# Fixing the order of every engine's queue in a planned mixture-of-experts kernel

## The chip, the cores and the metric

The kernel runs on one core of a Trainium2 chip. The metric is the time of one execution in microseconds on the device, taken as the median of several runs. A profile of one execution shows each engine's instructions: PE (TensorE, matrix products; its weight loads are listed as PEld), DVE (VectorE), ACT (ScalarE), POOL (GpSimd) and SP (SyncE, which here only issues transfers). Each engine works through its own queue in order; semaphores let it wait for the others.

## The reference

The input `x` is 16 sequences of 256 tokens with 256 features. Eight experts and one shared expert are all applied to every token, in float32, and the result is added to `x`:

```
g = einsum('bsd,edf->ebsf', h, Wg)            # E = 8, D = 256, F = 1024
u = einsum('bsd,edf->ebsf', h, Wu)
expert_outs = einsum('ebsf,efd->ebsd', silu(g) * u, Wd)
expert_output = einsum('be,ebsd->bsd', gating_probs, expert_outs)
shared = (silu(h @ Sg) * (h @ Su)) @ Sd
out = x + (1 - sg) * expert_output + sg * shared
```

There is no routing: the gate is a number for each sequence and expert, so the work is the same for any input.

## The kernel before, in words

The work is cut into 72 units `(e, half, g)`: nine experts (the shared one is the ninth), two halves of the 1024 hidden columns, and four groups `g` of four sequences. `g` runs innermost, so four units in a row use the same weights; I call the (expert, half) pair a weight set. There are 18 sets.

**One unit.** The up projection (`unit_up`) forms four token blocks times four column blocks for both weight matrices, `m = 0` (Wg) and `m = 1` (Wu). It does it with fewer products than the plain way. Four "diagonal" steps (`diagonal`) use the raw weights in the tile `wb` and the inputs in `xd`, and collect in the one PSUM bank `D`. Twelve "off-diagonal" steps (`offdiagonal`) use combined weights `wp` and combined inputs `xp`: one product goes to a bank `M`, the VectorE adds it to a sum `s` that GpSimd made from the diagonal results `p` and `q` (tiles `pq`), and writes the sum into a bank `X` (the row `X<-M,s`, which I call the seed); two more products are then added on top of the seed by TensorE. A finished bank goes through silu on ScalarE (`sg`), and the VectorE multiplies the `Wu` bank with it and with the gate `coef` into `h`. The down projection (`unit_down`) of the unit before runs between these products: seven products `dn` instead of eight, with weights `wd`, copied to `ev` by ScalarE and added to a total in HBM by a transfer that GpSimd issues.

**Weights.** `load_base` fetches one set's `wb` for one `m` in two transfers of 256 KB, `u` and `v`. Then GpSimd and VectorE rewrite parts of it in place (rows `wb<-wb`), and `make_pair` builds six `wp` tiles from each. There are four `wb` buffers, so a set's weights are fetched about one set ahead of their use.

**What sets the order.** The kernel does not issue its instructions directly. Every step is an `Op` with an engine, an estimated length, a lag (the time from its end until others may use its result), a rank, the steps that it depends on, and the buffers that it takes or uses. `Plan.run` walks through time with these estimates: an engine that is free takes the ready step of lowest rank, and TensorE is held to the exact rank order. A transfer's lag is `3 + kb / 150` us unless one is given; `load_base` gives 12 for all sets but the first. At the end `run` calls `emit` on all steps in the planned order. The recording layer below (the tile framework) then finds the data dependences and puts the instructions of each engine into an order of its own, by its own estimates; so the queues of the built program are not the planned ones. In the plan the load `v` depends on `u` and so stands 12 us later; in the built program only one other transfer stands between them on SP.

Of the kernel before, what the change touches and what calls it, by code (L numbers as in the profile page):

```python
# [46 lines left out]
class Plan:  # L47
# [18 lines left out]
    def add(self, engine, length, rank, emit, deps=(), new=(), uses=(), lag=None):  # L66
        lag = self.HOP if lag is None else lag
        op = Op(engine, length, lag, rank, emit, deps, list(new), list(uses))
        for b in [*op.new, *op.uses]:
            b.users += 1  # L70
        self.ops.append(op)
        return op

    def run(self):
        free = self.slots
        ready = {}
        serial = {id(op): n for n, op in enumerate(self.ops)}
        for op in self.ops:
            ready.setdefault(op.engine, [])
        at = {id(op): 0.0 for op in self.ops}  # L80
        idle = {e: 0.0 for e in ready}
        events = []
        for op in self.ops:
            if not op.missing:
                heapq.heappush(events, (0.0, serial[id(op)], 0, op))
        order = []
        left = len(self.ops)
        line = sorted((op.rank, serial[id(op)]) for op in self.ops if op.engine == "PE")
        at_line = 0
        turn = {tag: deque() for tag in free}  # L90
        for op in sorted(self.ops, key=lambda op: (op.rank, serial[id(op)])):
            for b in op.new:
                turn[b.tag].append(b)
        now = 0.0
        while left:
            while events and events[0][0] <= now + 1e-9:
                _, _, kind, op = heapq.heappop(events)
                if kind == 0:
                    heapq.heappush(ready[op.engine], (op.rank, serial[id(op)], op))
                elif kind == 1:  # L100
                    for b in [*op.new, *op.uses]:
                        b.users -= 1
                        if not b.users:
                            free[b.tag].append(b.tile)
            for e in ready:
                if idle[e] > now + 1e-9 or not ready[e]:
                    continue
                held, took = [], None
                while ready[e]:
                    item = heapq.heappop(ready[e])  # L110
                    if e == "PE" and item[:2] != line[at_line]:
                        held.append(item)
                        break
                    if all(free[b.tag] and turn[b.tag][0] is b for b in item[2].new) and all(
                        b.tile is not None for b in item[2].uses
                    ):
                        took = item[2]
                        for b in took.new:
                            b.tile = free[b.tag].popleft()
                            turn[b.tag].popleft()  # L120
                        break
                    held.append(item)
                for item in held:
                    heapq.heappush(ready[e], item)
                if took is None:
                    continue
                at_line += e == "PE"
                end = now + took.length
                idle[e] = end
                order.append(took)  # L130
                left -= 1
                heapq.heappush(events, (end, serial[id(took)], 2, took))
                heapq.heappush(events, (end + took.lag, serial[id(took)], 1, took))
                for a in took.after:
                    a.missing -= 1
                    t = end if a.engine == e == "PE" else end + took.lag
                    at[id(a)] = max(at[id(a)], t)
                    if not a.missing:
                        heapq.heappush(events, (at[id(a)], serial[id(a)], 0, a))
            if left:  # L140
                if not events:
                    raise RuntimeError("the plan has come to a stop")
                now = max(now, events[0][0])
        for op in order:
            op.emit()
        return now


@with_exitstack
def kernel(  # L150
# [28 lines left out]
    nc = tc.nc  # L179
# [8 lines left out]
    const = ctx.enter_context(tc.tile_pool(name="const", bufs=1))  # L188
    psum = ctx.enter_context(tc.tile_pool(name="psum", bufs=1, space=bass.MemoryType.PSUM))
    dram = ctx.enter_context(tc.tile_pool(name="dram", bufs=1, space=bass.MemoryType.DRAM))  # L190

    plan = Plan()
    add = plan.add
# [69 lines left out]
    def load(rank, dst, src, kb, deps=(), new=(), uses=(), lag=None):  # L263
        return add("SP", 0.6, rank, lambda: nc.sync.dma_start(dst(), src), deps, new, uses, lag=lag or 3 + kb / 150)  # L264

    def tt(engine, rank, o, a, b, op, n, deps, new=(), uses=(), slow=1.0):
        eng, length = (nc.vector, dve(n) * slow) if engine == "DVE" else (nc.gpsimd, pool(n))
        return add(engine, length, rank, lambda: eng.tensor_tensor(o(), a(), b(), op), deps, new, uses)  # L268
# [9 lines left out]
    def sources(e):  # L278
        return (Wg[e], Wu[e], Wd[e]) if e < E else (Sg, Su, Sd)
# [5 lines left out]
    def load_base(m, e, half, rank):  # L285
        b = Buf("wb", f"wb_{m}_{e}_{half}")
        src = [
            sources(e)[m][ts(part, P), ts(half, 4 * P)].rearrange("p (c q) -> p c q", q=P)
            for part in range(2)
        ]  # L290
        lag = None if rank < 0 else 12
        u = load(rank, lambda: b[:, :, 0, :], src[0], 256, [], [b], lag=lag)
        v = load(rank, lambda: b[:, :, 1, :], src[1], 256, [u], [], [b], lag=lag)
        ops = []
        for i, t in enumerate(POINTS):
            r, x_ = (lambda i=i: b[:, i, 1, :]), (lambda i=i: b[:, i, 0, :])
            if t == 0:
                op = v
            elif abs(t) == 1:
                op = tt("POOL", rank + 1, r, r, x_, ALU.add if t > 0 else ALU.subtract, P, [u, v], uses=[b])  # L300
            else:
                op = stt(rank + 1, r, x_, float(t), r, ALU.add, P, [u, v], uses=[b])
            ops.append(op)
        base[m, e, half], baseop[m, e, half] = b, (u, ops)
# [210 lines left out]
    def diagonal(n, m, unit, a, rank, pq, consume):  # L515

        e, half, g = unit
        w, (u, rops) = base[m, e, half], baseop[m, e, half]
        xb, xo = xd[g, a], xdop[g, a]
        name = f"{m}_{n}_{a}"  # L520
        bank = Buf("D", f"D_{name}")
        p_, q_ = pq
        new = a == 0
        ps, qs = [], []
        for h, i in enumerate((2 * a + 1, 2 * a)):
            ps.append(
                mm(
                    MM, rank + 1 / 8 + h / 100, lambda h=h: bank[:, h, :], lambda i=i: w[:, i, 0, :],
                    lambda i=i: xb[:, i % 2, :], h == 0, True, h == 1, [u, xo[i][0], *ps],
                    [bank] if h == 0 else [], [w, xb] if h == 0 else [w, xb, bank],  # L530
                )
            )

        sp = add(
            "ACT", act(2 * TB), rank + 0.3,
            lambda: nc.scalar.copy(p_[:, 2 - 2 * a : 4 - 2 * a, :], bank[:, :, :]), ps,  # L536
            [p_] if new else [], [bank] if new else [bank, p_],
        )
        for h, i in enumerate((2 * a + 1, 2 * a)):
            qs.append(  # L540
                mm(
                    MM, rank + 9 / 8 + h / 100, lambda h=h: bank[:, h, :], lambda i=i: w[:, i, 1, :],
                    lambda i=i: xb[:, 2 + i % 2, :], False, True, True, [rops[i], xo[i][1], sp],
                    [], [w, xb, bank],
                )
            )
        ops = {}
        for h, i in enumerate((2 * a + 1, 2 * a)):
            first = new and h == 0
            ops[i] = tt(  # L550
                "DVE", rank + 1.5, lambda i=i: q_[:, i, :], lambda h=h: bank[:, h, :],
                lambda i=i: p_[:, 3 - i, :], ALU.subtract, TB, [*qs, *ops.values()],
                [q_] if first else [], [bank, p_] if first else [bank, p_, q_],
            )
        consume(bank, [*ops.values()], rank + 1.6, [(2 * a + 1, 2 * a + 1), (2 * a, 2 * a)])
        return ops

    def offdiagonal(n, m, unit, k, rank, pq, pqops, consume):
# [322 lines left out]
    for n, unit in enumerate(units):  # L881
# [32 lines left out]
            finish(g, pieces, r0 + 2 * W + 1)  # L914
        else:
            unit_down(n, unit, hb, hops)
    plan.run()


# [36 lines left out]
```

## Time and profile before

| | us |
|---|---|
| runs | 2586.86, 2596.26, 2596.96; median 2596.26 |
| profiled execution, its own time | 2590.57 |
| its span, first to last instruction | 2588.8 |
| granted TensorE clock, mean | 0.997 |
| PE busy in the span | 2525.8 |
| PE weight loads, DVE, ACT, POOL busy | 1819.9, 1846.1, 788.8, 1800.1 |

The profiled execution took 1.8 us more than its span and 5.7 us less than the median of the runs. Busy time of PE is from modelled ends of matmuls, and includes matmuls that run while the clock is low; so a PE that is busy is not always at its best.

### The profile page before, as it was taken

The numbers are of one execution on the slowest core, as the hardware profiler recorded it, in microseconds if no ns is written. First come the engines' busy times: TensorE is split into PE (matmuls) and PEld (weight loads), VectorE is DVE, ScalarE is ACT, GpSimd is POOL, SyncE is SP. The second block draws the span as 40 slices with busy tenths as digits, with TensorE's granted clock in tenths as the row PEclk, the third lists the DMA queues.
The fourth block names the chain that finished last, engine by engine and source line by source line (L and its number), as shares of the span: only waits on it lengthen the run. The fifth ranks groups of instructions, "written<-read, shape, count | busy, mean of one in ns | idle before, by whom it ended". The sixth has DMA issues, their size and how long they took to land.

```text
span 2588.8 us, 30164 instructions
## 1 busy us (share of the span) xinstructions
PE 2525.8 (98%) x9644; PEld 1819.9 (70%) x9644; DVE 1846.1 (71%) x3272; ACT 788.8 (30%) x1367; POOL 1800.1 (70%) x1638
## 2 busy tenths in 40 slices
PE   8899999999999999999999999999999999999998
PEld 4667777767776777777676767777776777677766
DVE  6886766777676767676677767676766667776797
ACT  2333333333333333333333333333332333333310
POOL 5686767667676767676766757686767677676654
PEclk9999999999999999999999999999999999999999
DMA  6545666656666656666665665665666666666652
GB/s 196 197 162 154 171 157 164 162 158 164 166 157 164 157 158 169 154 170 156 163 161 161 161 166 157 167 154 158 171 154 164 161 165 158 163 163 177 174 188 90
DMA packets 179087, 421.47 MB, mean 163 GB/s; under 512 B 15057, under 2 KB 84193, under 8 KB 170225
## 3 DMA queue, kind: packets, MB, share of 16 engines
q1 hardware_dynamic: 159280, 294.70, 34.4%
q0 software_dynamic: 19648, 124.86, 26.2%
q8 instruction: 75, 1.23, 0.2%
q14 instruction: 84, 0.68, 0.1%
HBM read 276.90 MB, written 142.61 MB: 162 GB/s over the span
## 4 chain that ended last, share of the span: by engine, by line
PE 88%; DMA 6%; DVE 3%; issue 1%; POOL 1%; SPq 0%; ACT 0%; DVEq 0%; POOLq 0%
PE dn L509 31%; PE X L509 27%; PE D L509 17%; PE M L509 14%; DMA wb<-in_L_cond_Wg_dram 4%; DVE h L273 1%; DMA wb<-in_L_cond_Sg_dram 1%; DVE X L268 1%; DVE h L268 1%; SPq L264 0%; DMA total<-ev 0%; POOL wp L268 0%; PE dn L829 0%; DVE xp L268 0%; DMA wb<-in_L_cond_Wu_dram 0%
## 5 line engine op out<-in xcount | busy, mean ns | idle before, releaser
L268 POOL TENSOR_TENSOR s<-pq,pq 128x512 f32<-128x512 f32 x852 | 1191.3, 1402 | 483.2 <-DVE X L268 471.8
L509 PE MATMUL dn<-h,wd 128*128 128x512 f32 x1988 | 1018.0, 594 | 1.4 <-DVE xd L273 1.4
L509 PE MATMUL X<-xp,wp 128*128 128x256 f32 x3408 | 878.2, 380 | 37.0 <-DVE X L268 37.0
L268 DVE TENSOR_TENSOR X<-M,s 128x512 f32<-128x512 f32 x852 | 586.7, 692 | 435.4 <-PE M L509 227.9
L509 PEld LDWEIGHTS X<-xp,wp 128*128 128x128 f32 x3408 | 645.7, 190 | 254.5 <-issue 103.4
L509 PE MATMUL D<-xd,wb 128*128 128x256 f32 x2272 | 584.5, 380 | 2.6 <-ACT pq L536 2.2
L509 PEld LDWEIGHTS M<-xp,wp 128*128 128x128 f32 x1704 | 324.4, 190 | 346.0 <-issue 338.2
L509 PE MATMUL M<-xp,wp 128*128 128x256 f32 x1704 | 508.1, 380 | 0.1
L729 ACT COPY ev<-dn 128x512 f32<-128x512 f32 x476 | 278.8, 586 | 708.6 <-PE dn L509 708.6
L509 PEld LDWEIGHTS D<-xd,wb 128*128 128x128 f32 x2272 | 431.5, 190 | 67.3 <-ACT pq L536 3.9
L273 DVE SCALAR_TENSOR_TENSOR h<-X,coef,sg 128x256 f32<-128x256 f32 x852 | 375.9, 475 | 122.2 <-PE X L509 107.8
L268 DVE TENSOR_TENSOR h<-h,h 128x512 f32<-128x512 f32 x426 | 448.0, 1052 | 1.9
L509 PEld LDWEIGHTS dn<-h,wd 128*128 128x128 f32 x1988 | 377.6, 190 | 54.8 <-DVE xd L273 2.2
L607 ACT ACTIVATE sg<-X 128x512 f32<-128x512 f32 x434 | 259.1, 597 | 441.8 <-PE X L509 278.0
L536 ACT COPY pq<-D 128x512 f32<-128x512 f32 x284 | 166.5, 586 | 501.7 <-PE D L509 498.3
L268 DVE TENSOR_TENSOR pq<-D,pq 128x256 f32<-128x256 f32 x568 | 218.9, 416 | 25.5 <-PE D L509 25.3
L268 POOL TENSOR_TENSOR h<-h,h 128x512 f32<-128x512 f32 x142 | 197.8, 1393 | 3.6 <-DVE h L268 2.9
L743 POOL DMA_DIRECT2D total<-ev x128 | 112.8, 881 | 66.4 <-ACT ev L729 63.7
L268 POOL TENSOR_TENSOR wb<-wb 128x128 f32<-128x128 f32 x72 | 48.5, 684 | 129.1 <-DMA wb<-in_L_cond_Wg_dram 98.0
L273 DVE SCALAR_TENSOR_TENSOR h<-D,coef,sg 128x256 f32<-128x256 f32 x284 | 134.8, 475 | 0.0
L273 DVE SCALAR_TENSOR_TENSOR wp<-wb,wp 128x256 f32<-128x256 f32 x108 | 106.6, 998 | 29.9 <-POOL wp L268 24.0
L607 ACT ACTIVATE sg<-D 128x512 f32<-128x512 f32 x142 | 84.4, 594 | 98.5 <-DVE pq L268 98.5
(68 smaller groups left out, 561.1 us busy)
## 6 DMA issues: line engine op xcount, KB each, us to landing
xp<-keep_p SPq DMA_DIRECT2D x408, 384.0 KB, 3.9
total<-ev POOLq DMA_DIRECT2D x68, 1024.0 KB, 7.9
xd<-keep_d SPq DMA_DIRECT2D x136, 512.0 KB, 3.5
total<-ev POOLq DMA_DIRECT2D x68, 768.0 KB, 6.9
keep_p<-xp SPq DMA_DIRECT2D x24, 384.0 KB, 2.7
wb<-in_L_cond_Wg_dram SPq DMA_DIRECT2D x33, 256.0 KB, 5.5
wb<-in_L_cond_Wu_dram SPq DMA_DIRECT2D x33, 256.0 KB, 4.2
wd<-in_L_cond_Wd_dram SPq DMA_DIRECT2D x64, 128.0 KB, 2.7
```

What stands on the lines that cost most here:

```text
L268: return add(engine, length, rank, lambda: eng.tensor_tensor(o(), a(), b(), op), deps, new, uses)
L273: lambda: nc.vector.scalar_tensor_tensor(o(), a(), c() if callable(c) else c, b(), ALU.mult, op),
L509: lambda: nc.tensor.matmul(o(), w(), mv(), start=start, stop=stop, skip_group_check=onto),
L536: lambda: nc.scalar.copy(p_[:, 2 - 2 * a : 4 - 2 * a, :], bank[:, :, :]), ps,
L607: lambda: nc.scalar.activation(b[:, :, :], bank[:, :, :], AF.Silu), deps, [b], [bank],
L729: lambda ev=ev, at=at, bank=bank: nc.scalar.copy(ev[:, at, :], bank.tile.rearrange("p a t -> p (a t)")),
L743: nc.gpsimd.dma_start(total[g][part], ev[:, 0:k, :], accum_op=ALU.add)
```

## The change

Four things change. `Plan.run` returns the planned order, and the loop that emits it ties each instruction, by an order edge that carries no semaphore, to the one emitted before it on the same engine. The recording layer can then no longer exchange instructions of one engine; the planned order is the order of every queue. The lag of `load_base`'s transfers goes from 12 to 14 us. `v` no longer depends on `u`, so the plan issues both together. In `diagonal` the rank of the two subtractions that make `q` goes from `rank + 1.5` to `rank + 0.6`, and that of what follows them from `rank + 1.6` to `rank + 0.7`, which puts them ahead of other VectorE and ScalarE work that is ready at the same time.

```diff
@@ Plan.run
-        for op in order:
-            op.emit()
-        return now
+        return order
@@ tile_cond_moe_resid_kernel
+    same_queue = mybir.DependencyInfo(mybir.DependencyClass.NoSync, mybir.DependencyReason.DATA)
@@ load_base
-        lag = None if rank < 0 else 12
+        lag = None if rank < 0 else 14
         u = load(rank, lambda: b[:, :, 0, :], src[0], 256, [], [b], lag=lag)
-        v = load(rank, lambda: b[:, :, 1, :], src[1], 256, [u], [], [b], lag=lag)
+        v = load(rank, lambda: b[:, :, 1, :], src[1], 256, [], [], [b], lag=lag)
@@ diagonal
             ops[i] = tt(
-                "DVE", rank + 1.5, lambda i=i: q_[:, i, :], lambda h=h: bank[:, h, :],
+                "DVE", rank + 0.6, lambda i=i: q_[:, i, :], lambda h=h: bank[:, h, :],
                 lambda i=i: p_[:, 3 - i, :], ALU.subtract, TB, [*qs, *ops.values()],
                 [q_] if first else [], [bank, p_] if first else [bank, p_, q_],
             )
-        consume(bank, [*ops.values()], rank + 1.6, [(2 * a + 1, 2 * a + 1), (2 * a, 2 * a)])
+        consume(bank, [*ops.values()], rank + 0.7, [(2 * a + 1, 2 * a + 1), (2 * a, 2 * a)])
@@ end of the kernel
-    plan.run()
+    last = {}
+    for op in plan.run():
+        at = len(nc.cur_bb.bb.instructions)
+        op.emit()
+        for ins in nc.cur_bb.bb.instructions[at:]:
+            if ins.engine in last:
+                tc.add_manual_dep(ins, last[ins.engine], same_queue, reason="plan")
+            last[ins.engine] = ins.name
```

## The prediction

> **What bounds the kernel now.** I began with the page, whose first lines say which engine is full.
>
> ```profile
> PE 2525.8 (98%) x9644; PEld 1819.9 (70%) x9644; DVE 1846.1 (71%) x3272; ACT 788.8 (30%) x1367; POOL 1800.1 (70%) x1638
> ...
> PE 88%; DMA 6%; DVE 3%; issue 1%; POOL 1%; SPq 0%; ACT 0%; DVEq 0%; POOLq 0%
> ```
>
> TensorE is the bound, and the change removes no matmul. So I need the time that no order can take away. The chain of waits gives what one record costs when TensorE runs on (`PE X L509 x4` takes 0.86 us, `PE dn L509 x2` 0.86): 0.215 us for 256 columns, 0.43 for 512. With the counts of the page: 1988 dn x 0.43 + (3408 X + 2272 D + 1704 M) x 0.215 = 2442 us, and some 60 for the first and last units' own forms. That is about 2503 of a span of 2588.8: an order can win at most some 86 us. The windows show where they lie (us; PE, PEld, DVE, ACT, POOL busy; then clock, DMA share, GB/s).
>
> ```profile
> 0.00:160.00 160.00, 139.54 (x504) 89.78 (x505) 123.80 (x216) 46.60 (x92) 108.04 (x127) 0.98 0.57 190
> ...
> 290.00:404.00 114.00, 114.00 (x439) 83.08 (x438) 81.50 (x145) 36.26 (x63) 83.40 (x75) 1.00 0.58 155
> ...
> 2440.00:2589.00 149.00, 134.70 (x545) 96.31 (x543) 120.13 (x196) 22.24 (x38) 74.26 (x54) 1.00 0.50 153
> ```
>
> Within a weight set TensorE is never idle (114.00 of 114.00). The start loses 20.5 us, the end 14.3, and the rest is at the 15 places between 277 and 2243 where a new set's weights are fetched. Windows of 14 us around these places:
>
> ```profile
> 551.20:565.20 14.00, 11.96 (x42) 8.49 (x41) 8.34 (x16) 3.54 (x6) 7.21 (x8) 0.88 0.59 169
> 693.00:707.00 14.00, 12.01 (x50) 9.14 (x49) 9.71 (x17) 3.54 (x6) 8.77 (x9) 1.00 0.74 187
> ...
> 1393.20:1407.20 14.00, 12.06 (x42) 8.42 (x42) 9.03 (x17) 3.54 (x6) 7.97 (x8) 0.88 0.71 186
> ...
> sum 210.00, PE 181.57 PEld 136.40 DVE 143.50 ACT 53.09 POOL 129.15; mean PE 12.10 PEld 9.09 DVE 9.57 ACT 3.54 POOL 8.61
> ```
>
> The list of waits names what TensorE lacked, and what its supplier lacked; the timeline of one place shows the order of events.
>
> ```profile
> PE X L509 <- DVE X L268: 37.0, 22, 2.8
> ...
> POOL wb L268 <- DMA wb<-in_L_cond_Wg_dram: 98.0, 13, 11.6
> DVE wb L273 <- DMA wb<-in_L_cond_Wg_dram: 89.6, 15, 7.2
> ```
>
> ```profile
> 546.14 0.38 SPq L264 DMA_DIRECT2D wb<-in_L_cond_Wg_dram  x1
> ...
> 548.36 0.70 DVE L268 TENSOR_TENSOR X<-M,s 128x512 f32<-128x512 f32 x1 [1.38 <-POOL s L268]
> 555.46 0.29 DVE L273 SCALAR_TENSOR_TENSOR wb<-wb 128x128 f32<-128x128 f32 x1 [6.40 <-DMA wb<-in_L_cond_Wg_dram]
> 555.67 0.87 DVE L273 SCALAR_TENSOR_TENSOR h<-X,coef,sg 128x256 f32<-128x256 f32 x2
> 556.46 1.29 DVE L268 TENSOR_TENSOR X<-M,s 128x512 f32<-128x512 f32 x2
> ...
> 557.20 1.73 PE L509 MATMUL X<-xp,wp 128*128 128x256 f32 x4 [2.04 <-DVE X L268]
> ```
>
> The second load of Wg is issued at 546.14. VectorE reaches the rewrite of these weights at 549.06, 2.9 us later, and stands there until the load lands, 9.2 us after its issue. GpSimd does the same. The new weights are for the next set, and sets are 140 us apart, but the seed `X<-M,s` is behind them in VectorE's queue, and TensorE, which had work for 6 us, runs dry.
>
> **The change part by part.** *The tie with the longer lag, and `v` issued beside `u`.* In the planned order, which is now each queue's order, I counted the matmuls between the second load of a set and its first use. For Wg: 28 of 256 columns and 8 of 512 before VectorE's rewrite (28 x 0.43 + 8 x 0.86 = 18.9 us), and 28.4 before GpSimd's. For Wu, 14.6 and 21.1. The slowest landing of a `wb` load in the trace is 10.0 us. So the rewrite no longer waits, and nothing is queued behind a wait.
>
> [...] The trace has a DMA share of 0.70 to 0.80 in most of the 15 windows, against 0.58 within a set. [...]
>
> What the 15 places cost: 210.00 - 181.57 = 28.4 us without a matmul. After a gap the first group of four takes 1.13 us instead of 0.86 in the chain: 13 x 0.27 = 3.5. And twice the clock fell: 2 x (1 - 0.88) x 14 = 3.4. [...] The rows show 0.88 after gaps near 2 us, so I count it: 35.3. I keep 3 us as still lost in one place or another: -32.
>
> *The start.* `v` of the first set moves up from the tenth transfer on SP to the second, so GpSimd's rewrite, which started at 14.5 us, can start near 6. VectorE now makes two `wp` tiles ahead of the first `h`, where it made six; TensorE's `PE M L509 <- DVE h L273: 4.5, 2, 3.3` should go. Against it: 512 KB more stand ahead of the last two inputs (2.2 us at the first window's 234 GB/s; TensorE waited for them at 11.5), and `oms<-coef` is now VectorE's first step. It needs a transfer that landed at 9.75 (issued at 2.35, 7.4 to landing), and with its 0.42 and 0.71 us it delays the first copy from 8.1 to 10.9. I take these two, which overlap, at 1.5: net -3. For the rest of the first 160 us the trace shows no such order; VectorE is 87% to 96% busy there. Bounds: all of the remaining waits for VectorE gone (-8), or as much lost (+6). I take -1, since the work is the same.
>
> *The diagonal's ranks.* No instruction is added: 568 subtractions (416 ns) and 284 products (475 ns) move up in VectorE's queue, and 142 silus in ScalarE's. TensorE waits only 2.6 us in all for bank `D`, so a gain is bounded by that. The cost is bounded by what is delayed: up to 2 x 0.42 + 2 x 0.48 = 1.8 us for a seed behind them. Within a set VectorE waits for TensorE's `M` (227.9 us in all), so it is ahead of TensorE and covers this: 0.
>
> *Order edges* carry no semaphore and add no instruction: 0. *SP's queue:* the four `wd` loads of a set now stand in one block (an issue like the one at 546.14 takes 0.38 us), with the `xp` loads behind them. Those are planned 19 us ahead (median) and land in 3.8 (8.3 at most): 0. *The end:* the same reading of the totals; a store that lands after 9.5 us is planned with 8, so a wait there stays. Bounds -5 and +5; 0.
>
> **Sum.** 2590.6 (the profiled execution) - 32 - 3 - 1 = 2554.6. The median of the runs is 5.7 us above that execution, the fastest run 3.7 below it; I add 2: **2557 us**, 1.5% less than the median.
>
> **The rivals.** *Slower: the fixed queue makes VectorE late in every unit.* The diagonal's four steps come ahead of a seed 284 times (4 a unit, 71 units). It decides as soon as more than (36 + 13) / 284 = 0.17 us a time is not covered. At 0.25 it gives 2590 + 71 - 36 = 2625. For it: a fixed queue can't step around a step that is late, and TensorE had 98%. Against it: 114.00 of 114.00 within a set, with VectorE waiting for TensorE. 10%.
> *Partly given back.* GpSimd has about 14 us of weight work a set (48.5 + 105.0 + 94.7 us in its groups over 18 sets); freed of its wait it may hold up the sums `s` that a seed needs. If about half of the 32 us stay as such waits: 2575. 12%.
> *Nothing moves.* The plan's estimates are off where it matters, and its own order waits at the same places or at the start, for the 36 us that it saves: 2590. 8%.
>
> **How the numbers follow.** The main case has 70%; its own range is 2541 to 2570. About 0.5% (13 us) is what a measurement of this kernel can tell from no change. Faster by more than that: main and partly, 0.82. Within: 0.09, the last rival and the edge of another. Slower: 0.09. The range from 2536 (35 at the sets, 12 at the start, 7 at the end) to 2592 leaves out most of the slow rival and the ends of the others.
>
> **What would show it.** Right: no wait of VectorE or GpSimd on `wb<-in_L_cond_Wg_dram` over 1 us after 160 us; `PE X L509 <- DVE X L268` below 8 us; PE 13.8 or more in the 14 us windows, with clock 1.00. The start: no gap of 3 us before the first `M` products near 27 us. Wrong: PE below 113.5 of 114 within a set (the slow rival), or GpSimd's `s` as the releaser of seeds at the sets (partly given back).

## The result, and the profile after

| | before | after |
|---|---|---|
| median of five runs (us) | 2594.71 (2586.86 to 2596.96) | 2561.45 (2560.55 to 2563.84) |
| ratio, 95% interval | | 0.9877 [0.986, 0.9893] |
| profiled execution (us) | 2590.57 | 2560.55 |
| its span | 2588.8 | 2558.8 |
| clock, mean | 0.997 | 0.997 |

The change takes 1.2% off. The profiled span falls by 30.0 us. The windows say where (after: us; PE, PEld, DVE, ACT, POOL busy; clock, DMA share, GB/s; the last window ends with the span, as it did before):

```profile
0.00:160.00 160.00, 138.09 (x496) 89.91 (x497) 116.29 (x208) 45.58 (x90) 98.13 (x116) 0.97 0.54 182
290.00:404.00 114.00, 114.00 (x438) 82.68 (x436) 86.45 (x151) 36.75 (x65) 81.10 (x79) 1.00 0.59 155
2410.00:2559.00 149.00, 133.34 (x534) 96.04 (x533) 119.53 (x192) 20.93 (x36) 69.69 (x52) 0.98 0.49 152
```

Within a set TensorE is still never idle. The start loses 21.9 us (20.5 before) at a clock of 0.97 (0.98); the end loses 15.7 (14.3) at 0.98 (1.00). Both ends are therefore a little worse. All of the gain is at the 15 places where a set's weights are fetched. Windows of 14 us that begin 3 us behind the issue of the first load (those of the prediction begin 7 to 8 us behind it):

```profile
546.80:560.80 14.00, 14.00 (x55) 10.26 (x54) 7.45 (x15) 4.83 (x9) 6.64 (x7) 1.00 0.93 232
684.60:698.60 14.00, 14.00 (x56) 10.26 (x55) 7.40 (x15) 4.88 (x9) 6.64 (x7) 1.00 0.94 230
...
sum 210.00, PE 210.00 PEld 154.07 DVE 111.54 ACT 72.83 POOL 98.88; mean PE 14.00 PEld 10.27 DVE 7.44 ACT 4.86 POOL 6.59
```

TensorE fills 210.00 of 210.00 us, where it had 181.57, and the clock is 1.00 in each. These windows end ahead of the rewrites, but over the whole stretch from 160 to 2240 us TensorE is busy 2079.80 of 2080.00 us too. The timeline of the place that the prediction showed, again after the change, has no wait in it:

```profile
543.75 2.12 SPq L264 DMA_DIRECT2D wb<-in_L_cond_Wg_dram  x2
...
565.70 0.70 DVE L273 SCALAR_TENSOR_TENSOR wb<-wb 128x128 f32<-128x128 f32 x1
```

Both loads are issued by 545.87, and VectorE comes to their rewrite 20 us later, not 2.9 us later. The list of waits (us in total, times, longest) agrees:

```profile
PE dn L401 <- DVE xd L273: 8.1, 3, 4.2
PE X L509 <- DVE X L268: 7.4, 5, 2.6
POOL wb L268 <- DMA wb<-in_L_cond_Wg_dram: 2.6, 1, 2.6
```

TensorE's wait for seeds falls from 37.0 to 7.4 us. GpSimd's wait for Wg falls from 98.0 to 2.6, once, at the start; VectorE's, 89.6 before, is gone from the list. What grows most on TensorE is `PE dn L401 <- DVE xd L273`, from 4.0 to 8.1 us, and this is at the start.

### The profile page after: what moved, and what is told of

The parts are those of the page before. It is cut to its first block, busy times and chain, and to the rows that moved or that the text cites. A ratio compares the mean times of both kernels' runs of the same rounds, so it can differ in the third digit from the quotient of the medians.

```text
span 2558.8 us, 30286 instructions
## 1 busy us (share of the span) xinstructions
PE 2521.2 (99%) x9644; PEld 1822.6 (71%) x9644; DVE 1894.3 (74%) x3272; ACT 778.3 (30%) x1367; POOL 1721.5 (67%) x1638
## 3 DMA queue, kind: packets, MB, share of 16 engines
q8 instruction: 76, 1.25, 0.2%
## 5 line engine op out<-in xcount | busy, mean ns | idle before, releaser
L268 POOL TENSOR_TENSOR s<-pq,pq 128x512 f32<-128x512 f32 x852 | 1147.9, 1376 | 523.1 <-DVE X L268 502.9
L273 DVE SCALAR_TENSOR_TENSOR h<-X,coef,sg 128x256 f32<-128x256 f32 x852 | 394.8, 478 | 214.3 <-PE X L509 163.8
L268 DVE TENSOR_TENSOR h<-h,h 128x512 f32<-128x512 f32 x426 | 468.6, 1126 | 0.0
L268 POOL TENSOR_TENSOR wp<-wb 128x128 f32<-128x128 f32 x216 | 140.4, 661 | 0.0
L273 DVE SCALAR_TENSOR_TENSOR h<-D,coef,sg 128x256 f32<-128x256 f32 x284 | 134.5, 474 | 0.0
L273 DVE SCALAR_TENSOR_TENSOR wp<-wb,wp 128x256 f32<-128x256 f32 x108 | 88.3, 819 | 0.0
```

Of the source, the lines that this page charges most:

```text
L273: lambda: nc.vector.scalar_tensor_tensor(o(), a(), c() if callable(c) else c, b(), ALU.mult, op),
```

## Experiments

Times are medians; each ratio is to runs of the kernel before on the same chip. Diffs are against the changed kernel unless they say otherwise.

**The edges alone (`tie_only`), against the kernel before:** `load_base` and `diagonal` are as they were.

```diff
-        for op in order:
-            op.emit()
-        return now
+        return order
...
+            if ins.engine in last:
+                tc.add_manual_dep(ins, last[ins.engine], same_queue, reason="plan")
+            last[ins.engine] = ins.name
```

> The kernel before with the order edges alone: v still depends on u, the lag is 12, and the diagonal's ranks are the old ones. Theory 1 (the recording layer put the rewrite of the weights too early in the queues; the planned order cures it): in this plan the first rewrite stands at least 12.5 us of matmuls behind the second load, and the slowest landing measured is 10.3 us, so the waits at the weight sets go and the time is 2555 to 2572 us. Theory 2 (the pairing of u and v and the longer lag do it): 2585 to 2597. Theory 3 (the diagonal's ranks do it): 2585 to 2597.

Measured: 2560.12 us, ratio 0.987 [0.9855, 0.9884]. The edges give all of the gain. With the landing time of 12 us that the plan had already, the planned order keeps the rewrites far enough behind their loads. TensorE's wait for seeds is as short as in the changed kernel:

```profile
PE X L509 <- DVE X L268: 5.8, 4, 2.8
```

**The loads alone (`loads_only`), against the kernel before:** no edges.

```diff
-        lag = None if rank < 0 else 12
+        lag = None if rank < 0 else 14
...
-        v = load(rank, lambda: b[:, :, 1, :], src[1], 256, [u], [], [b], lag=lag)
+        v = load(rank, lambda: b[:, :, 1, :], src[1], 256, [], [], [b], lag=lag)
```

> The kernel before with the lag of 14 and with v freed from u, but no order edges and the old ranks. Theory 1: the recording layer still orders the queues by its own estimates, the rewrite stands about 3 us behind the load again, PE X waits about 2 us at each of 15 sets: 2580 to 2600 us. Theory 2: 2555 to 2575.

Measured: 2592.99 us, ratio 0.9996 [0.9985, 1.0008]: nothing. Both waits stay:

```profile
DVE wb L273 <- DMA wb<-in_L_cond_Wg_dram: 89.3, 15, 7.9
PE X L509 <- DVE X L268: 39.2, 23, 3.6
```

The queues are not the plan's, so the plan's estimate of a landing does not reach them.

**The old ranks of the diagonal (`ranks_old`):**

```diff
-                "DVE", rank + 0.6, lambda i=i: q_[:, i, :], lambda h=h: bank[:, h, :],
+                "DVE", rank + 1.5, lambda i=i: q_[:, i, :], lambda h=h: bank[:, h, :],
...
-        consume(bank, [*ops.values()], rank + 0.7, [(2 * a + 1, 2 * a + 1), (2 * a, 2 * a)])
+        consume(bank, [*ops.values()], rank + 1.6, [(2 * a + 1, 2 * a + 1), (2 * a, 2 * a)])
```

> The changed kernel with the diagonal's ranks put back to 1.5 and 1.6. Theory 1: the sets stay free of waits, TensorE is full within a set in either case, 2556 to 2567 us. Theory 3 (the ranks carry the gain): over 2580.

Measured: 2564.42 us, ratio 0.9886 [0.9871, 0.99], against 0.9877 with the new ranks. The ranks' 3 us lie inside the intervals.

**The same fixed queues with the rewrite put close behind its load (`early_rewrite`).** The plan is told that a set's load lands 2 us after its issue. By the planned order TensorE then has 2.6 us of matmuls between the load and VectorE's rewrite.

```diff
-        lag = None if rank < 0 else 14
+        lag = None if rank < 0 else 2
```

> The changed kernel, its order edges included, with a lag of 2 us for the weight loads in place of 14: VectorE's rewrite then stands 2.6 us of matmuls behind the load of Wg, as it did in the kernel before (2.9 us). Theory 1: the wait comes back although the queues are fixed, VectorE stands 5 to 7 us at each of 15 sets and TensorE loses about 2 us there, 2583 to 2600 us. Rival (it is the fixed order as such that helps, by fewer semaphore waits on VectorE and GpSimd): 2556 to 2568.

Measured: 2622.08 us, ratio 1.0112 [1.0094, 1.013], slower than the kernel before. From its timeline:

```profile
556.72 2.13 SPq L264 DMA_DIRECT2D wb<-in_L_cond_Wg_dram  x2
...
568.43 0.29 DVE L273 SCALAR_TENSOR_TENSOR wb<-wb 128x128 f32<-128x128 f32 x1 [7.05 <-DMA wb<-in_L_cond_Wg_dram]
...
570.17 1.68 PE L509 MATMUL X<-xp,wp 128*128 128x256 f32 x4 [2.69 <-DVE X L268]
```

The wait that the change removed is back at the same place: VectorE stands 7.05 us, then TensorE 2.69. So a fixed order gains nothing by being fixed; the distance between load and rewrite in it decides. This kernel loses more than the kernel before, and more than I expected. Its trace says where. From 160 to 2300 us TensorE is idle for 39.7 us; the kernel before lost 28.4 at the sets, the changed kernel loses 0.2. The clock also falls at nine of the sets, where it fell at two before: the group of four at 570.17 takes 1.68 us, where 1.13 follows a gap at the full clock, and the 14 us from 569 have a clock of 0.88. Over the span the mean clock is 0.990 against 0.997 in the changed kernel; 0.007 of the span is an estimated 18 us. Idle time and clock make up about 58 of the 66 us between the two spans (2625.0 and 2558.8).

**Edges on VectorE's and GpSimd's queues only (`tie_dve_pool`), and on VectorE's only (`tie_dve`):**

```diff
+            if ins.engine not in (mybir.EngineType.DVE, mybir.EngineType.Pool):
+                continue
```

> The changed kernel, but order edges are laid on VectorE's and GpSimd's queues alone; TensorE, ScalarE and SyncE are ordered by the recording layer again. Theory 1 (what counts is how far behind a weight load VectorE's and GpSimd's rewrites stand in their own queues): 2555 to 2567 us, no wait of either on wb<-in_L_cond_Wg_dram over 1 us after 160 us, and PE 13.8 or more in the 14 us windows at the sets. Theory 2 (the gain needs the matmul order too, since TensorE's order is what kept the layer's order and the plan's apart): 2580 to 2592, with waits of TensorE on X or D in every set.

```diff
+            if ins.engine != mybir.EngineType.DVE:
+                continue
```

> The changed kernel, but order edges are laid on VectorE's queue alone; GpSimd's is the recording layer's. Theory 1 (either engine standing at a load in its queue is enough to starve TensorE, since a seed needs GpSimd's s as well): GpSimd waits some 7 to 11 us for wb<-in_L_cond_Wg_dram at most sets, VectorE then waits for s, and the time is 2572 to 2590. Theory 2 (only VectorE's wait reached TensorE; GpSimd's s is made far enough ahead of its use to hide 10 us): 2556 to 2566, with GpSimd's wait still in the list but PE near 14.00 in the windows at the sets.

Measured: with both queues tied 2551.01 us, ratio 0.9832 [0.9817, 0.9847], better than with all tied, and 4 us below the range that I gave. With VectorE's alone 2634.88 us, ratio 1.0158 [1.0143, 1.0173]: far slower than either theory allowed. It is not the wait at the load: GpSimd still stands at Wg for 64.3 us in 10 waits, but VectorE's wait for `s` is 68.5 us, as with both queues tied (68.8), and TensorE's wait for seeds is only 10.5. In its place stands another wait, about two a set:

```profile
PE D L509 <- ACT sg L607: 50.0, 33, 3.6
```

The mean clock is 0.990 (0.999 with both tied); by the difference an estimated 24 us go there. One of the waits:

```profile
283.24 0.86 POOL L743 DMA_DIRECT2D total<-ev  x1
...
284.86 5.83 DVE L268 TENSOR_TENSOR h<-h,h 128x512 f32<-128x512 f32 x1
...
285.08 1.54 POOL L268 TENSOR_TENSOR h<-h,h 128x512 f32<-128x512 f32 x1
...
289.18 0.95 POOL L268 TENSOR_TENSOR wp<-wp,wb 128x256 f32<-128x256 f32 x1
...
290.61 0.41 DVE L268 TENSOR_TENSOR pq<-D,pq 128x256 f32<-128x256 f32 x1
...
291.70 1.13 PE L509 MATMUL D<-xd,wb 128*128 128x256 f32 x4 [2.25 <-ACT sg L607]
```

VectorE's `h<-h,h` takes 0.68 us when it is alone. Here it takes 5.83 us. It starts 0.8 us behind an accumulating transfer that GpSimd issued, and ends when the GpSimd instructions behind that issue, which follow each other without a pause, have run out (290.13). The step `pq<-D` waits behind it, the silu for `pq`, TensorE for the silu. In this kernel 30 VectorE operations take over 4 us, about two a set; with GpSimd's queue tied as well there is one, at the start, and in the kernel before there is one. My reading is that the layer's order of GpSimd's queue puts the weight work right behind the issue, while VectorE's fixed queue cannot step round. Length alone is no loss: in the changed kernel 64 VectorE operations between 160 and 2400 us take 2.2 to 4 us, none did before, and TensorE stays full. The next experiments ask what holds the operation.

**The first set's plain stores issued by SyncE (`sp_store`).** The changed kernel has the same event twice in its start (at 101.63 and 143.06 us). The first stands ahead of TensorE's longest wait:

```profile
100.54 0.57 POOL L741 DMA_DIRECT2D total<-ev  x1 [2.65 <-ACT ev L729]
...
101.63 4.18 DVE L273 SCALAR_TENSOR_TENSOR xp<-xd,xp 128x256 f32<-128x256 f32 x1
...
104.27 1.26 POOL L268 TENSOR_TENSOR h<-h,h 128x512 f32<-128x512 f32 x1
...
110.71 0.65 PE L401 MATMUL dn<-ident,xio 128*128 128x128 f32 x4 [4.19 <-DVE xd L273]
```

```diff
-                        nc.gpsimd.dma_start(total[g][part], ev[:, 0:k, :])
+                        nc.sync.dma_start(total[g][part], ev[:, 0:k, :])
...
-                    "POOL", 0.9, r + 0.1, store, [*evops, totalop.get((g, part))], uses=[ev], lag=8.0
+                    "SP" if first else "POOL", 0.6 if first else 0.9, r + 0.1, store, [*evops, totalop.get((g, part))], uses=[ev], lag=8.0
```

> The changed kernel, but the first set's stores of the totals (plain writes of ev, one for each total) are issued by SyncE and not by GpSimd. In the changed kernel two VectorE operations right behind such an issue take 4.18 us instead of 0.4 to 0.9, and TensorE has gaps near them (110.7 and 150 us). Theory 1 (GpSimd's issue of a plain store holds VectorE's operation up): both long operations are gone and the time falls by 2 to 6 us, to 2555 to 2560. Theory 2 (the length is due to something else at that place, or the gaps near it come from the order): long operations stay at 99 to 105 and 140 to 145 us, or go without any gain; 2560 to 2563.

Measured: 2559.54 us, ratio 0.9864 [0.9848, 0.9881]. Both operations of 4.18 us are gone (the longest near the first is 1.79). TensorE's longest wait for `xd` falls from 4.2 to 2.4 us. PE is 141.43 in the first 160 us against 138.09, but the clock is lower, 0.96 against 0.97 there and 0.95 against 0.98 in the last 149 us, and of the 3.3 us little arrives: 1.9 us less than the changed kernel, inside the intervals. So the long operations go with the issue, but a gain in time is not shown.

**The first step of VectorE and the last inputs (`head_order`):**

```diff
-    coef_op = add("DVE", 0.8, -2, make_coef)
+    coef_in = add("COEF", 0.01, -3, lambda: None, lag=9.7)
+    coef_op = add("DVE", 0.8, -2, make_coef, [coef_in])
...
-        v = load(rank, lambda: b[:, :, 1, :], src[1], 256, [], [], [b], lag=lag)
+        v = load(rank, lambda: b[:, :, 1, :], src[1], 256, [u] if rank < 0 else [], [], [b], lag=lag)
```

> The changed kernel, but in the plan the gate's step on VectorE (oms<-coef) is held until 9.7 us, behind the first copies, and in the first weight set alone v depends on u again, as it did before the change. Theory 1 (the predicted -4 us of the start was lost because VectorE's first step waits 8.3 us for the gate's transfer and the last inputs come later): first copies near 8.3 instead of 10.1 us, the first products near 13.2 instead of 15, and 1.5 to 3 us less in all: 2558 to 2560. Theory 2 (the start is bounded by VectorE's amount of work in the first 160 us, so an earlier first product is given back by gaps later): 0, within 1.5 us of the changed kernel, with PE in the first 160 us still 137.5 to 139.

Measured: 2560.18 us, ratio 0.9868 [0.9853, 0.9882]. The first copy moves from 10.11 to 8.55 us and the first `X` product from 14.98 to 14.06, but PE in the first 160 us is 138.06 against 138.09, at a clock of 0.95 against 0.97. What comes earlier is given back before 160 us, as the second theory said; that VectorE's amount of work is the reason is not shown by it.

**What holds VectorE (`port`, then `port_issue`).** Two small programs, which compute nothing of the reference, measured by one profile each. Part of the first (the second operation of VectorE is the one that is timed):

```diff
+                nc.scalar.copy(t, last)
+                for i in range(n):
+                    nc.gpsimd.tensor_tensor(g[i], t, big[:, 512:1024], ALU.mult)
...
+                nc.vector.tensor_tensor(first, lead, t, ALU.mult)
...
+                    nc.vector.tensor_tensor(o, first, big[:, 1024:1536], ALU.mult)
```

> A small program of its own: none of the reference is computed, the output holds products of the input. In each trial GpSimd is given 0, 1, 2, 4 or 8 products of 128x512 from SBUF in a row, and VectorE, just behind their start, one operation of 128x512: two operands in SBUF (tensor_tensor, or the same with a scalar), one operand in PSUM and one in SBUF, or one operand in SBUF. Theory 1 (VectorE's operation with both operands in SBUF can't start until GpSimd's run of back-to-back instructions ends, which is what made h<-h take 4.2 to 7.2 us in the kernel with VectorE's edges alone, and xp<-xd,xp 4.18 us at 101.63 us of the changed kernel): with two SBUF operands it takes about 0.7 us alone, and about 1.3 us more for each further GpSimd product, some 10 us behind 8; with an operand in PSUM, or a single operand, it stays near 0.6 to 0.7. Theory 2 (it waits for one GpSimd instruction at most): never more than about 2 us, whatever the run. Theory 3 (the length came from the DMA issue or the stores nearby): 0.7 in every trial.

Measured: with two SBUF operands 0.69 us alone and 1.13 to 1.20 beside 1, 2, 4 or 8 products alike; with one in PSUM 0.69 throughout; with a single SBUF operand 0.43 alone and 0.86 to 0.93 beside GpSimd, which no theory of mine had. The first theory was wrong and the second held: beside back-to-back products alone VectorE's operation took at most 0.51 us more (1.20 against 0.69), and no more beside eight than beside one. The second program puts the issue of a transfer first:

```diff
+        if issue == "plain":
+            emit(nc.gpsimd.dma_start, total, ev)
+        elif issue == "accum":
+            emit(nc.gpsimd.dma_start, total, ev, accum_op=ALU.add)
         for i in range(n):
             emit(nc.gpsimd.tensor_tensor, g[i], t, big[:, 512:1024], ALU.mult)
```

> A second small program of its own, without any of the reference: as the first, but in each trial GpSimd may issue a transfer of 128x2048 to HBM first (none, a plain store, or an accumulating one), then 0, 1, 4 or 8 products of 128x512; VectorE starts its operation with two SBUF operands behind one, two or four short PSUM operations of 0.7 us. In two last trials VectorE's operation has one operand in PSUM. In the kernel with VectorE's edges alone and in the changed kernel, the operations of over 2.2 us nearly all start within 4 us of such an issue and end 4.7 to 6.6 us behind its end. Theory 1 (an issue from GpSimd with products queued behind it holds VectorE's two-operand operation until most of those have run): no more than 1.2 us without an issue, 0.7 to 1.2 with an issue and no product behind it, and 3 to 6 us with an issue and 4 or 8 products. Theory 2 (the issue alone holds it, products or not): 3 to 6 us with 0 products too. Theory 3 (neither; what held it was something else of the kernel, such as the semaphores between GpSimd's own rewrites): never over 2 us.

Three trials of its timeline, all with 8 products: no issue; a plain store; the store again, with VectorE's operand in PSUM:

```profile
32.16 10.25 POOL L31 TENSOR_TENSOR g<-ev,big 128x512 f32<-128x512 f32 x8 [0.73 <-ACT ev L31]
32.73 1.25 DVE L31 TENSOR_TENSOR none<-big,ev 128x512 f32<-128x512 f32 x1
...
109.29 0.58 POOL L31 DMA_DIRECT2D total<-ev  x1 [1.64 <-ACT ev L31]
109.64 10.60 DVE L31 TENSOR_TENSOR plain<-big,ev 128x512 f32<-128x512 f32 x1
109.89 9.79 POOL L31 TENSOR_TENSOR g<-ev,big 128x512 f32<-128x512 f32 x8
...
296.48 9.80 POOL L31 TENSOR_TENSOR g<-ev,big 128x512 f32<-128x512 f32 x8
296.93 0.68 DVE L31 TENSOR_TENSOR bnk<-bank,ev 128x512 f32<-128x512 f32 x1
```

Behind an issue VectorE's operation lasts 0.68 us with no product behind it, 2.04 with one, 5.73 with four and 10.60 with eight. Started later, behind four short operations, it takes 3.53 with four and 8.41 with eight: it ends with the run each time, 0.5 to 0.6 us behind the last product. An accumulating transfer does the same (6.02 and 10.88). The first theory holds, and more strongly than I wrote it: VectorE waits for the whole run, up to the eight products tried. Its bound of 1.2 us without an issue was too low (1.25 to 1.73 while products ran).

**All edges but TensorE's (`tie_no_pe`), and the smallest version (`dve_pool_min`: the kernel before plus edges on VectorE and GpSimd):**

```diff
+            if ins.engine == mybir.EngineType.PE:
+                continue
```

> The changed kernel with the edges on every queue but TensorE's. Theory 1 (the 10 us between the changed kernel and the one with edges on VectorE and GpSimd alone are TensorE's: tied, it stands behind a step whose input is late at the start and at the end, where the layer's order lets another matmul go first): 2549 to 2554 us. Theory 2 (they come from ScalarE's or SyncE's edges, late copies or late transfers): 2558 to 2563.

> The kernel before with one edit: edges on VectorE's and GpSimd's queues. Lag, the place of v and the diagonal's ranks are as before the change. Theory 1 (only where the two engines' rewrites stand counts; the rest of the change carries nothing): 2548 to 2555 us. Theory 2 (the ranks or the longer landing time carry part of it once TensorE's order is the layer's): 2556 to 2575.

Measured: 2554.49 us, ratio 0.9865 [0.9848, 0.9881], and 2546.56 us (2546.17 to 2549.27), ratio 0.9835 [0.982, 0.9849], the fastest of all. The smallest version lies 1.4 us below the range that I gave. It has the ratio of `tie_dve_pool` (0.9832), so the lag, `v` and the ranks add nothing there either. Its two ends:

```profile
0.00:160.00 160.00, 146.56 (x539) 94.43 (x540) 128.67 (x226) 50.75 (x97) 111.67 (x131) 1.00 0.58 200
...
2395.00:2544.00 149.00, 137.21 (x548) 97.78 (x546) 122.48 (x196) 22.50 (x39) 73.05 (x54) 0.99 0.50 154
```

Against the changed kernel TensorE has 8.5 us more work done in the first 160 us and 3.9 more in the last 149; that is 12.3 of the 14.4 us between the spans. TensorE's own edges are probably part of it: without them its wait at `dn<-xd` falls from 8.1 to 4.8 us, the last window rises from 133.34 to 136.03, and the first from 138.09 to 141.70. But `tie_no_pe` missed its range by half a microsecond, its interval overlaps the changed kernel's, and versions with TensorE tied reach 141.43 in the first window (`sp_store`) and 135.72 in the last (`head_order`). How much is TensorE's, and how the rest divides between ScalarE's and SyncE's edges, was not settled.

## Why the prediction held

**The sets: right.** The step said 35.3 us at the 15 places, of which 3 might stay lost. All of it came: 28.4 us of idle time to 0.00, no slow first group, no fallen clock. The clock term was worth counting: before, the granted clock was 0.88 at two of the places, after gaps of 2.04 and 1.94 us; with the gaps gone it is 1.00 in all 15 windows. The length of a gap alone does not decide it, though: the other 13 gaps, up to 2.79 us, left the clock at 1.00. The cause is shown from two sides: `loads_only` leaves the waits and the time, `early_rewrite` brings them back inside the fixed queues.

**The landing: right.** The DMA share in the windows after is between 0.91 and 0.98, but they lie closer to the loads; in the 14 us from the first load's issue, at the place shown, it is 0.83, against 0.81 before. The slowest landing of a `wb` load is 10.3 us, against 10.0 before. With 20 us between load and rewrite neither matters.

**The start: the term that was mis-sized.** I took -4 us; it is +1.4 of idle time and about 1.6 of clock (0.01 of 160 us; the column has two digits, so it may be nothing or twice that). GpSimd's rewrite did start early (5.50 us) and the gap near 27 us is gone. The cost that I held against it was larger: VectorE's first copy came at 10.11, and the first `X` product at 14.98 instead of 13.22. Then new waits ended at 57.6, 89.1 and 110.7 us (3.3, 2.4 and 4.2 us). `head_order` shows that undoing the first cost alone brings nothing by 160 us. Part of the last (1.8 us of it in `sp_store`) goes back to the held operation, which the prediction did not know. Two pairs of runs that differ only in the loads and the ranks say more (one profile each). With these as they were before the change, PE in the first 160 us is 140.66, not 138.09 (`tie_only`), and 146.56, not 144.00 (`dve_pool_min` against `tie_dve_pool`); the old ranks alone give 138.32 (`ranks_old`). So the change to the loads, which I took as a gain of 3, seems to cost 2 to 3 us there. Why is open: `head_order` puts the first set's `v` back and has 138.06. I also read VectorE's load there too high: before, it is 85% to 96% busy from 50 us on, and only 73% between 25 and 50 us.

**The end: a little low.** I took 0 within bounds of 5; it is +1.4 us of idle time and about 3 of clock. Two versions whose TensorE is free, `tie_no_pe` and `dve_pool_min`, have 136.0 and 137.2 of 149 there.

**Ranks and edges: right for the ranks, incomplete for the edges.** The page's counts of the five engines are unchanged, as I said, but an edge also takes away the choice of going round a late step. I gave that to VectorE as a rival. The runs hint at TensorE instead, at the start and the end, where `tie_no_pe` has 3.6 and 2.7 us more of its work done; with VectorE alone tied, the rival came true by another mechanism than mine.

The sum: the step's -36 from 2590.6 gave 2554.6 for the profiled execution, which is 2560.55. The sets brought 3 more than taken, the start 7 less and the end about 4 less by these figures; they add up to -28, and the span moved by 30.0; the remaining 2 us are not placed. For the median I gave 2557 us, and it is 2561.45. Part of this is luck: the sets' surplus hid a quarter of what the two ends lost. The rivals fell as they should: TensorE has 114.00 of 114.00 within a set, and the seeds' wait for GpSimd's `s` fell from 198.5 to 72.4 us.

## What to carry to other kernels

When a bound engine stops at regular places, look for an instruction that waits for a transfer far ahead of its need, and ask what stands behind it in its queue; moving it to 20 us behind the load was worth some 35 us here, while a better estimate of the load alone was worth nothing. Fix the order of the queues where a wait does harm, together where they feed each other (VectorE and GpSimd: -42 us; VectorE alone: +42), and try leaving the other queues free: the versions that tied these two and left TensorE's free were 7 to 15 us faster than the one with all tied, though it was not settled whose edges cost this. On GpSimd, look at what runs straight behind the issue of a transfer, since VectorE may be held for all of it (10.60 us behind an issue and eight products in the small program).

## What the runs showed of the hardware

In the small programs (128x512, float32) a VectorE operation with two SBUF operands that started behind a transfer's issue on GpSimd, while GpSimd's back-to-back products ran, ended 0.5 to 0.6 us behind the last of them: it took 10.60 us behind an issue and eight products, 0.68 behind an issue and none. Without the issue it took at most 1.73 us, beside products of 1.3, and 0.69 alone. With an operand in PSUM it took 0.68 behind an issue and eight products. Why an issue makes this difference was not tried.
